# Attention kernel: q's and k's weights loaded by SP, idle products from ones, ACT's parts of the forms after the step's exponentials, another tail for the last group

## The chip, the cores and the metric

The kernel runs on one core of one Trainium2 chip. The metric is the device time of one launch in microseconds (us), median of several runs. Its engines: PE (TensorE, matrix products, with its weight loads PEld), DVE (VectorE), ACT (ScalarE), POOL (GpSimd) and SP (SyncE, which only issues transfers here). Each engine works through its own list of instructions in order; semaphores hold an instruction back until another engine or a transfer has got far enough.

## The reference

Four images of 64 x 64 positions and 256 channels. Without the parts that are not called:

```python
q = jnp.einsum('bwhc,cd->bwhd', x, Wq) + bq      # 128 channels
k = jnp.einsum('bwhc,cd->bwhd', x, Wk) + bk      # 128 channels
v = jnp.einsum('bwhc,cd->bwhd', x, Wv) + bv      # 256 channels
pq, pk, pv = (t.reshape(B, -1, N) for t in (q, k, v))   # N = 4096
energy = jnp.einsum('bcn,bcm->bnm', pq, pk)      # 4096 x 4096 for each image
attention = jax.nn.softmax(energy, axis=-1)
out = jnp.einsum('bcm,bnm->bcn', pv, attention)
return gamma * out.reshape(B, W, H, C) + x
```

All of it is float32.

## The kernel before

The large products run on PE in a faster type (fp32r) that keeps fewer bits, so each float32 operand is split into parts, here called its forms: an upper part h, made by ACT with a multiplication by a number just under 1, and two more, made by DVE out of h and the operand (`scalar_tensor_tensor`). `halved` (L260) makes the forms of q and k, `halve_v` (L288) those of v (vh, vl, vd), `upper` and `halves` those of the exponentials.

For each image there is first a projection phase of 16 tiles i. `transposed(i)` loads a tile of x by SP, transposes it on PE (L124), and ACT copies it out (L130). `project_qk(b, i)` (L271) makes q and k on PE (L137), DVE adds the bias (qks, L146), POOL stores q to DRAM (L275), `halved` makes k's forms (ACT L263, DVE L266), and POOL stores these (L279). `project_v` does the same for v (PE L158, ACT L167 and L292, DVE L296); the v forms of the last two tiles are left for the steps.

Then follow 128 steps u: 16 groups g of 256 columns n, and in each group 8 steps t, each over 512 rows m. A step u works on several stages at once:

- `energy(b, u + 3, k)` for k = 0 and 1: six products on PE into the PSUM banks sa and sb (L330; two banks each, taken in turn), then two exponentials on ACT, x from sa and y from sb (L334).
- `join(b, u + 2)`: x = x * y on DVE (L344); `upper(b, u + 2)`: h on ACT (L349). Both stand between the energies of k = 0 and those of k = 1.
- `halves(b, u + 1)`: l and d on DVE (L355, L358).
- `attend(b, u)`: 24 products on PE into the accumulators acc (two banks a0, a1, of h and l) and the shared bank bb (of d) (L380). vh and vl carry two columns of ones, so that column C of an accumulator is the sum of the exponentials, Z.

At each step with `ahead % 8 == 5` q's forms for the next group are made (`halve_q`); in steps 1 and 3 of an image the v forms that were left. Both are generators in two pieces: the ACT part (L263, L292) stands right after the energies of k = 0, ahead of h; the DVE parts (L266, L296) stand at the end of the step, after `halves`.

After a group's last step ACT takes the accumulators out into o (L391), and `finish` does the rest in pieces, one for each `proceed()`: DVE takes Z, its reciprocal times gamma and adds bb (L404 to L406); ACT scales o (L409); PE transposes o into ot (L417); DVE adds it to x (L421); POOL stores the result (L422). `begin` and the list of `proceed()` calls fix where each piece stands between the other work. At the end of an image the pieces of its last group fall into the next image's first projections:

```python
            if b + 1 < B:
                proceed()
                images[b + 1].transposed(1)
                proceed()
                project_qk(b + 1, 0)
```

In the order of PE's list the next image's transposes of tile 2, the transposes ot of the last group, and q and k of tile 1 then follow one another.

The very last group has its own tail, `finish_last` (L440): Z from both accumulators, factors r and ra on DVE, ACT scales bb, DVE adds the scaled accumulators (L455), PE transposes, DVE adds to x (L465), SP stores. `guard` (L424) checks that all Z lie between two limits and writes the flag `again`; every engine reads it at L561 and would run a general path, which these inputs do not take.

At the start, ACT issues the loads of Wq and Wk (L90, L91), POOL those of the biases, Wv and gamma, SP those of x. PE makes 12 idle transposes of the identity (L199), which POOL has to build first.

Of the kernel before, what the change touches and what calls it, by code (L numbers as in the profile page):

```python
# [9 lines left out]
F32 = mybir.dt.float32  # L10
# [3 lines left out]
ALU = mybir.AluOpType  # L14
# [6 lines left out]
def kernel(  # L21
# [65 lines left out]
    ones = const.tile([P, P], F32, name="ones")  # L87
    nc.vector.memset(ones, 1.0)
    wqk_sb = const.tile([P, KC, 2 * C2], F32, name="wqk_sb")
    nc.scalar.dma_start(wqk_sb[:, :, :C2], wq.rearrange("(k p) d -> p k d", p=P))  # L90
    nc.scalar.dma_start(wqk_sb[:, :, C2:], wk.rearrange("(k p) d -> p k d", p=P))  # L91
    bqk_sb = const.tile([P, 2 * C2], F32, name="bqk_sb")
    nc.gpsimd.dma_start(bqk_sb[:, :C2], bq.partition_broadcast(P))
    nc.gpsimd.dma_start(bqk_sb[:, C2:], bk.partition_broadcast(P))
# [100 lines left out]

    with tc.tile_pool(name="ps_w", bufs=1, space=PSUM) as ps_w:
        wp = ps_w.tile([P, P], F32, name="wp")
        for _ in range(12):
            nc.tensor.transpose(wp, ident, ident)  # L199

    with ExitStack() as fast:
        fast.enter_context(tc.manual_schedule())
# [57 lines left out]
        def halved(f, x):  # L260

            h = f[:, :, 0, :]
            nc.scalar.activation(h, x, AF.Identity, scale=UPPER / 64)  # L263
            yield
            for j, s, op in ((1, -64.0, ALU.add), (2, 64.0 * (1.0 + E), ALU.subtract)):
                nc.vector.scalar_tensor_tensor(  # L266
                    f[:, :, j, :], h.bitcast(F32), s, x, ALU.mult, op
                )
            yield

        def project_qk(b, i):  # L271
            images[b].qk(i)
            x = now["qk"]
            for s in range(2):
                nc.gpsimd.dma_start(qd[b, i // 2 + NG // 2 * s][:, i % 2, :], x[:, s, :C2])  # L275
            f = kpool.tile([P, 2, 3, P], F32R, tag="f", name=f"f_{b}_{i}", bufs=2)
            for _ in halved(f, x[:, :, C2:]):
                pass
            nc.gpsimd.dma_start(kf[b, i // 2][:, i % 2], f.rearrange("p s j d -> p s (j d)"))  # L279

        def project_v(b, i):
            images[b].v(i)
            units[b, "v4", i] = now["v4"]
            if i < NI - 2:
                for _ in halve_v(b, i):
                    pass

        def halve_v(b, i):  # L288
            v4 = units.pop((b, "v4", i))
            m = slice(2 * i, 2 * i + 2)  # L290
            h = vh[:, m, :C]
            nc.scalar.activation(h, v4, AF.Identity, scale=UPPER * E)  # L292
            yield

            for t, f in ((vl, 1.0 / E), (vd, 1.0 / E + 1.0)):
                nc.vector.scalar_tensor_tensor(  # L296
                    t[:, m, :C], h.bitcast(F32), -f, v4, ALU.mult, ALU.add
                )
            yield

        def load_q(b, g):
            t = work.tile([P, NJ, P], F32, tag="qr", name=f"qr_{b}_{g}", bufs=1)
# [2 lines left out]

        def halve_q(b, g):
            t = work.tile([P, 3, NJ, P], F32R, tag="q", name=f"q_{b}_{g}")
            loads[b, "q", g] = t
            yield from halved(t.rearrange("p f j d -> p j f d"), loads.pop((b, "qr", g)))

        def load_k(b, u):
            if u < STEPS:
# [80 lines left out]
        def factors(b, g, gamma):  # L393

            r = work.tile([P, 2, NJ], F32, tag="r", name=f"r_{b}_{g}")
            nc.vector.reciprocal(r[:, 0, :], zall[:, b * NG + g, :])
            nc.vector.tensor_tensor(r[:, 0, :], r[:, 0, :], gamma.to_broadcast([P, NJ]), ALU.mult)
            return r[:, 0, :], r[:, 1, :]

        def finish(b, g, o, bb, xr):  # L400
            yield
            yield

            nc.vector.tensor_copy(zall[:, b * NG + g, :], o[:, :, C])  # L404
            r, _ = factors(b, g, gam1)
            nc.vector.tensor_tensor(o[:, :, :C], o[:, :, :C], bb, ALU.add)  # L406
            yield
            for j in range(NJ):
                nc.scalar.activation(  # L409
                    o[:, j, :C], o[:, j, :C], AF.Identity, scale=r[:, j : j + 1]  # L410
                )
            yield
            yield
            tp = ps_t.tile([P, 2, NB], F32, tag="t", name=f"ot_{b}_{g}")
            for s in range(2):
                for j in range(NJ):
                    nc.tensor.transpose(  # L417
                        tp[:, s, j * P : (j + 1) * P], o[:, j, s * P : (s + 1) * P], ident
                    )
            yield  # L420
            nc.vector.tensor_tensor(xr, xr, tp, ALU.add)  # L421
            nc.gpsimd.dma_start(ov[b, g], xr)  # L422

        def guard():  # L424

            z = zall.rearrange("p n j -> p (n j)")
            ok = ppool.tile([P, 4, NB], F32, tag="y", name="ok")[:, 0, : B * NG * NJ]
            nc.vector.tensor_scalar(ok, z, Z_LOW, None, ALU.is_ge)
            nc.vector.scalar_tensor_tensor(ok, z, Z_HIGH, ok, ALU.is_le, ALU.mult)
            yield  # L430
            nc.vector.tensor_reduce(zs, ok, AX.X, ALU.min)
            nc.vector.tensor_scalar(zs, zs, 0.5, None, ALU.is_lt)
            zp = ps_s.tile([P, 1], F32, tag="b", name="zp")
            nc.tensor.matmul(zp, ones, zs, start=True, stop=True)
            yield
            nc.vector.tensor_copy(again, zp)
            yield
            yield

        def finish_last(b, g, xr):  # L440

            for j in range(NJ):
                a = now["acc"][j]
                nc.vector.tensor_copy(zall[:, b * NG + g, j : j + 1], a[:, C : C + 1])
            r, ra = factors(b, g, gam)
            check = guard()
            nc.vector.tensor_scalar(ra, r, 1.0 + E, None, ALU.mult)
            o = work.tile([P, NJ, C + 2], F32, tag="o", name=f"o_{b}_{g}")
            tps = []
            for j in range(NJ):  # L450
                next(check)
                nc.scalar.activation(
                    o[:, j, :C], now["bb"][:, j, :], AF.Identity, scale=r[:, j : j + 1]
                )
                nc.vector.scalar_tensor_tensor(  # L455
                    o[:, j, :C], now["acc"][j][:, :C], ra[:, j : j + 1], o[:, j, :C], ALU.mult, ALU.add
                )
                tp = (ps_t, ps_s)[j].tile([P, 2, P], F32, tag="ta"[j], name=f"ot_{b}_{g}_{j}")
                for s in range(2):
                    nc.tensor.transpose(tp[:, s, :], o[:, j, s * P : (s + 1) * P], ident)  # L460
                tps.append(tp)
            for j in range(NJ):
                next(check)
                n = slice(j * P, (j + 1) * P)
                nc.vector.tensor_tensor(xr[:, :, n], xr[:, :, n], tps[j], ALU.add)  # L465
            nc.sync.dma_start(ov[b, g], xr)

        def begin(b, i):

            if i == 5:  # L470
                load_q(b, 0)
            if i == 9:
                for _ in halve_q(b, 0):
                    pass
            if i in (4, 6, 8):
                load_k(b, i // 2 - 2)
            if i >= 10:
                energy(b, (i - 10) // 2, i % 2)
            if i in (12, 14):
                join(b, i // 2 - 6)  # L480
            if i in (13, 15):
                upper(b, i // 2 - 6)
                load_k(b, i // 2 - 3)

        image(0)
        for b in range(B):
            pr = images[b]
            if b == 0:
                now["banks"] = energies
                pr.transposed(0)  # L490
                pr.transposed(1)
                project_qk(b, 0)
            for i in range(1, NI):
# [13 lines left out]
            for u in range(STEPS):  # L507
# [182 lines left out]
```

## Time and profile before

| | us |
|---|---|
| median of 3 runs | 2453.45 (2453.05 to 2455.39) |
| the profiled execution | 2453.05 |
| its span, first to last instruction | 2451.3 |
| PE, PEld busy | 2438.7, 2408.0 |
| DVE, ACT, POOL busy | 2099.0, 1795.2, 424.5 |

The mean TensorE clock that was granted is 0.999 of full speed. A row of the timeline has the start in us from the span's start, the duration, the engine, the line, the operation, out<-in with shapes, how many instructions are merged, and in brackets how long the engine stood idle before and what released it. An ACT or DVE instruction can start a little before the last one has ended.

### The profile page before, as it was taken

To read this page: it belongs to the slowest core of one execution; us is meant where nothing else is said; L and a number is where in the kernel's file an instruction comes from. 1 tells how busy PE (TensorE), PEld (TensorE's weight loads), DVE (VectorE), ACT (ScalarE), POOL (GpSimd) and SP (SyncE) were. 2 spreads that over 40 slices of the span, in tenths; PEclk is the share of its full clock that TensorE was granted. 3 is DMA by queue.
4 is the path that set the end of the run, shared out by engine and by line. 5 is a ranking of instruction groups with operands and counts; after the bars stand their busy time and mean duration, and the time that the engine had idled before them with its cause. 6 is when DMAs were issued, how large, how long until landed. Compare 5 with 4: busy or idle time off the path is not lost.

```text
span 2451.3 us, 50024 instructions
## 1 busy us (share of the span) xinstructions
PE 2438.7 (99%) x19982; PEld 2408.0 (98%) x19982; DVE 2099.0 (86%) x2314; ACT 1795.2 (73%) x3201; POOL 424.5 (17%) x781
## 2 busy tenths in 40 slices
PE   9999999999999999999999999999999999999998
PEld 8999999999899999999989999999998999999998
DVE  5988888888698888888869888888886988888887
ACT  5777777776677777777667777777766777777775
POOL 4211111111411111111141111111114111111110
PEclk9999999999999999999999999999999999999999
DMA  7766666665776666666477666666647766666663
GB/s 234 224 202 209 204 207 202 202 215 153 235 221 197 210 203 208 208 197 213 141 243 226 203 203 202 208 210 201 206 140 248 223 204 201 204 207 210 203 202 111
DMA packets 137407, 498.92 MB, mean 204 GB/s; under 512 B 15536, under 2 KB 57264, under 8 KB 137168
## 3 DMA queue, kind: packets, MB, share of 16 engines
q0 software_dynamic: 92320, 453.17, 60.0%
q1 hardware_dynamic: 44304, 42.22, 5.5%
q8 instruction: 160, 2.62, 0.4%
q14 instruction: 79, 0.65, 0.1%
q10 hardware_dynamic: 544, 0.26, 0.0%
HBM read 445.25 MB, written 50.33 MB: 202 GB/s over the span
## 4 chain that ended last, share of the span: by engine, by line


## 5 line engine op out<-in xcount | busy, mean ns | idle before, releaser
L334 ACT ACTIVATE x<-sa 128x512 f32<-128x512 f32 x1024 | 612.2, 598 | 516.1 <-PE sa L330 514.0
L344 DVE TENSOR_TENSOR x<-x,y 128x1024 f32<-128x1024 f32 x512 | 626.2, 1223 | 234.4 <-ACT y L334 234.4
L330 PE MATMUL sa<-q,k 128*128 128x256 f32 x4096 | 735.4, 279 | 0.0
L358 DVE SCALAR_TENSOR_TENSOR d<-h,x 128x1024 fp32r<-128x1024 f32 x512 | 623.3, 1217 | 0.0
L355 DVE TENSOR_TENSOR l<-x,h 128x1024 fp32r<-128x1024 f32 x512 | 623.2, 1217 | 0.0
L330 PEld LDWEIGHTS sa<-q,k 128*128 128x128 f32 x4096 | 619.4, 188 | 0.4
L334 ACT ACTIVATE y<-sb 128x512 f32<-128x512 f32 x1024 | 615.7, 601 | 0.0
L380 PE MATMUL a<-vh,h 128*128 128x258 f32 x4096 | 574.4, 283 | 0.0
L380 PE MATMUL a<-vl,l 128*128 128x258 f32 x4096 | 572.8, 282 | 0.0
L330 PE MATMUL sb<-q,k 128*128 128x256 f32 x2048 | 567.1, 277 | 0.0
L380 PE MATMUL bb<-vd,d 128*128 128x256 f32 x4096 | 558.6, 279 | 0.0
L314 POOL DMA_DIRECT2D k<-kf x512 | 279.1, 545 | 1573.3 <-PE sb L330 1548.3
L349 ACT ACTIVATE h<-x 128x1024 fp32r<-128x1024 f32 x512 | 543.8, 1062 | 8.3 <-DVE x L344 7.8
L380 PEld LDWEIGHTS a<-vl,l 128*128 128x128 f32 x4096 | 525.3, 189 | 0.0
L380 PEld LDWEIGHTS a<-vh,h 128*128 128x128 f32 x4096 | 522.9, 189 | 0.0
L380 PEld LDWEIGHTS bb<-vd,d 128*128 128x128 f32 x4096 | 515.1, 188 | 0.0
L330 PEld LDWEIGHTS sb<-q,k 128*128 128x128 f32 x2048 | 384.5, 188 | 0.1
L137 PE MATMUL qk<-wqk_sb,xts 128*128 128x256 f32 x512 | 121.0, 379 | 0.0
L158 PE MATMUL v<-xts,wv_sb 128*128 128x256 f32 x512 | 120.3, 379 | 0.0
L158 PEld LDWEIGHTS v<-xts,wv_sb 128*128 128x128 f32 x512 | 97.3, 190 | 13.2
L137 PEld LDWEIGHTS qk<-wqk_sb,xts 128*128 128x128 f32 x512 | 92.3, 190 | 10.0
L275 POOL DMA_DIRECT2D qd<-qks x128 | 69.2, 549 | 179.8 <-DVE qks L146 170.6
(56 smaller groups left out, 864.4 us busy)
## 6 DMA issues: line engine op xcount, KB each, us to landing
k<-kf POOLq DMA_DIRECT2D x512, 768.0 KB, 4.7
x<-in_x_dram SPq DMA_DIRECT2D x128, 256.0 KB, 3.9
kf<-f POOLq DMA_DIRECT2D x64, 384.0 KB, 4.0
out_dram<-x POOLq DMA_DIRECT2D x63, 256.0 KB, 2.5
qd<-qks POOLq DMA_DIRECT2D x128, 64.0 KB, 3.0
qr<-qd SPq DMA_DIRECT2D x64, 128.0 KB, 3.6
wv_sb<-in_L_conv_Wv_dram POOLq DMA_DIRECT2D x1, 256.0 KB, 5.7
out_dram<-x SPq DMA_DIRECT2D x1, 256.0 KB, 3.8
```

The source lines that it names most:

```text
L137: nc.tensor.matmul(qk[:, s, :], self.xt[i][:, k, s, :], wqk_sb[:, k, :], start=(k == 0), stop=(k == KC - 1),)
L158: nc.tensor.matmul(vp[:, eh, :], wv_sb[:, k, eh * P : (eh + 1) * P], self.xt[i][:, k].rearrange("p s a -> p (s a)"), start=(k == 0), stop= ...
L275: nc.gpsimd.dma_start(qd[b, i // 2 + NG // 2 * s][:, i % 2, :], x[:, s, :C2])
L314: nc.gpsimd.dma_start(t.rearrange("p (i s) f d -> p i s (f d)", s=2), kf[b, u % NU])
L330: nc.tensor.matmul(to[:, i], kt[:, 2 * k + i, f, :], q[:, f], start=first, stop=last)
L334: nc.scalar.activation(to[:, 2 * k : 2 * k + 2, :], sp.rearrange("p i j d -> p i (j d)"), AF.Exp, scale=scale,)
L344: nc.vector.tensor_tensor(x, x, y, ALU.mult)
L349: nc.scalar.activation(h, units[b, u], AF.Identity, scale=UPPER)
L355: nc.vector.tensor_tensor(l, x, h.bitcast(F32), ALU.subtract)
L358: nc.vector.scalar_tensor_tensor(d, h.bitcast(F32), 1.0 + E, x, ALU.mult, ALU.subtract)
L380: nc.tensor.matmul(out_, left[:, i, j * P : (j + 1) * P], right[:, m, : out_.shape[1]], start=(t == i == 0 and (left is h or left is d and ...
```

## The change

- SP issues the loads of Wq and Wk, after its first tile of x and before its second.
- PE's idle work is 7 matrix products of the tile of ones with itself instead of the 12 transposes, and two more of them between the transposes of the first and the second tile.
- `halved` and `halve_v` are plain functions: ACT's part and DVE's parts of q's and v's forms are made together at the end of the step, so that ACT's part comes after both pairs of exponentials.
- At the end of an image `project_qk(b + 1, 0)` comes ahead of the second `proceed()`, the one in which ACT scales o.
- In the last group ACT scales the two accumulators, DVE scales and adds bb; the comparison of the guard is one operation on POOL (`max` and `min`) and one on DVE (`is_equal`), and its product zp comes after the transposes.

```diff
-    nc.scalar.dma_start(wqk_sb[:, :, :C2], wq.rearrange("(k p) d -> p k d", p=P))
-    nc.scalar.dma_start(wqk_sb[:, :, C2:], wk.rearrange("(k p) d -> p k d", p=P))
...
         wp = ps_w.tile([P, P], F32, name="wp")
-        for _ in range(12):
-            nc.tensor.transpose(wp, ident, ident)
+        for _ in range(7):
+            nc.tensor.matmul(wp, ones, ones, start=True, stop=True)
...
             h = f[:, :, 0, :]
             nc.scalar.activation(h, x, AF.Identity, scale=UPPER / 64)
-            yield
             for j, s, op in ((1, -64.0, ALU.add), (2, 64.0 * (1.0 + E), ALU.subtract)):
...
-            yield
...
             nc.scalar.activation(h, v4, AF.Identity, scale=UPPER * E)
-            yield
...
+            halved(t.rearrange("p f j d -> p j f d"), loads.pop((b, "qr", g)))
             loads[b, "q", g] = t
-            yield from halved(t.rearrange("p f j d -> p j f d"), loads.pop((b, "qr", g)))
...
             ok = ppool.tile([P, 4, NB], F32, tag="y", name="ok")[:, 0, : B * NG * NJ]
-            nc.vector.tensor_scalar(ok, z, Z_LOW, None, ALU.is_ge)
-            nc.vector.scalar_tensor_tensor(ok, z, Z_HIGH, ok, ALU.is_le, ALU.mult)
-            yield
+            nc.gpsimd.tensor_scalar(ok, z, Z_LOW, Z_HIGH, ALU.max, ALU.min)
+            nc.vector.tensor_tensor(ok, ok, z, ALU.is_equal)
             nc.vector.tensor_reduce(zs, ok, AX.X, ALU.min)
-            nc.vector.tensor_scalar(zs, zs, 0.5, None, ALU.is_lt)
             zp = ps_s.tile([P, 1], F32, tag="b", name="zp")
             nc.tensor.matmul(zp, ones, zs, start=True, stop=True)
-            yield
-            nc.vector.tensor_copy(again, zp)
...
+            return zp
...
         def finish_last(b, g, xr):
 
+            r = work.tile([P, 2, NJ], F32, tag="r", name=f"r_{b}_{g}")
+            o = work.tile([P, NJ, C + 2], F32, tag="o", name=f"o_{b}_{g}")
+            acc, bb = now["acc"], now["bb"]
             for j in range(NJ):
-                a = now["acc"][j]
-                nc.vector.tensor_copy(zall[:, b * NG + g, j : j + 1], a[:, C : C + 1])
-            r, ra = factors(b, g, gam)
-            check = guard()
-            nc.vector.tensor_scalar(ra, r, 1.0 + E, None, ALU.mult)
-            o = work.tile([P, NJ, C + 2], F32, tag="o", name=f"o_{b}_{g}")
+                rj, raj, z = r[:, 0, j : j + 1], r[:, 1, j : j + 1], acc[j][:, C : C + 1]
+                nc.vector.reciprocal(rj, z)
+                nc.vector.tensor_tensor(raj, rj, gam1, ALU.mult)
+                nc.scalar.activation(o[:, j, :C], acc[j][:, :C], AF.Identity, scale=raj)
+                nc.vector.tensor_tensor(rj, rj, gam, ALU.mult)
+            for j in range(NJ):
+                nc.vector.tensor_copy(zall[:, b * NG + g, j : j + 1], acc[j][:, C : C + 1])
             tps = []
             for j in range(NJ):
-                next(check)
-                nc.scalar.activation(
-                    o[:, j, :C], now["bb"][:, j, :], AF.Identity, scale=r[:, j : j + 1]
-                )
                 nc.vector.scalar_tensor_tensor(
-                    o[:, j, :C], now["acc"][j][:, :C], ra[:, j : j + 1], o[:, j, :C], ALU.mult, ALU.add
+                    o[:, j, :C], bb[:, j, :], r[:, 0, j : j + 1], o[:, j, :C], ALU.mult, ALU.add
                 )
...
+            zp = guard()
             for j in range(NJ):
-                next(check)
                 n = slice(j * P, (j + 1) * P)
                 nc.vector.tensor_tensor(xr[:, :, n], xr[:, :, n], tps[j], ALU.add)
+                if j == 0:
+                    nc.vector.tensor_scalar(again, zp, P - 0.5, None, ALU.is_lt)
             nc.sync.dma_start(ov[b, g], xr)
...
                 now["banks"] = energies
+                pr.load(0)
+                nc.sync.dma_start(wqk_sb[:, :, :C2], wq.rearrange("(k p) d -> p k d", p=P))
+                nc.sync.dma_start(wqk_sb[:, :, C2:], wk.rearrange("(k p) d -> p k d", p=P))
                 pr.transposed(0)
+
+                wp = ps_t.tile([P, P], F32, tag="t", name="wp1")
+                for _ in range(2):
+                    nc.tensor.matmul(wp, ones, ones, start=True, stop=True)
                 pr.transposed(1)
...
-                beside = []
-                if ahead // NU + 1 < NG and ahead % NU == 5:
-                    beside.append(halve_q(b, ahead // NU + 1))
-                if u in (1, 3):
-                    beside.append(halve_v(b, NI - 2 + u // 2))
                 for k in range(2):
                     if ahead < STEPS:
                         energy(b, ahead, k)
-                    if k == 0:
-                        for forms in beside:
-                            next(forms)
                     if k == 0 and u + 2 < STEPS:
                         join(b, u + 2)
                         upper(b, u + 2)
...
                 if u + 1 < STEPS:
                     halves(b, u + 1)
-                for forms in beside:
-                    next(forms)
+                if ahead // NU + 1 < NG and ahead % NU == 5:
+                    halve_q(b, ahead // NU + 1)
+
+                if u in (1, 3):
+                    halve_v(b, NI - 2 + u // 2)
                 attend(b, u)
...
                 proceed()
                 images[b + 1].transposed(1)
+                project_qk(b + 1, 0)
                 proceed()
-                project_qk(b + 1, 0)
```

More of the change, by code (lines that the diff above doesn't have):

```diff
@@ L276, in project_qk @@
             f = kpool.tile([P, 2, 3, P], F32R, tag="f", name=f"f_{b}_{i}", bufs=2)
-            for _ in halved(f, x[:, :, C2:]):
-                pass
+            halved(f, x[:, :, C2:])
             nc.gpsimd.dma_start(kf[b, i // 2][:, i % 2], f.rearrange("p s j d -> p s (j d)"))
@@ L284, in project_v @@
             if i < NI - 2:
-                for _ in halve_v(b, i):
-                    pass
+                halve_v(b, i)
         def halve_v(b, i):
@@ L391, in attend @@
                     nc.scalar.activation(o[:, j, :], acc[j], AF.Identity, scale=1.0 + E)
[L393 to L398, printed above, removed]
         def finish(b, g, o, bb, xr):
@@ L404, in finish @@
             nc.vector.tensor_copy(zall[:, b * NG + g, :], o[:, :, C])
-            r, _ = factors(b, g, gam1)
+            r = work.tile([P, 2, NJ], F32, tag="r", name=f"r_{b}_{g}")[:, 0, :]
+            nc.vector.reciprocal(r, zall[:, b * NG + g, :])
+            nc.vector.tensor_tensor(r, r, gam1.to_broadcast([P, NJ]), ALU.mult)
             nc.vector.tensor_tensor(o[:, :, :C], o[:, :, :C], bb, ALU.add)
@@ L427, in guard @@
             ok = ppool.tile([P, 4, NB], F32, tag="y", name="ok")[:, 0, : B * NG * NJ]
-            nc.vector.tensor_scalar(ok, z, Z_LOW, None, ALU.is_ge)
-            nc.vector.scalar_tensor_tensor(ok, z, Z_HIGH, ok, ALU.is_le, ALU.mult)
-            yield
+            nc.gpsimd.tensor_scalar(ok, z, Z_LOW, Z_HIGH, ALU.max, ALU.min)
+            nc.vector.tensor_tensor(ok, ok, z, ALU.is_equal)
             nc.vector.tensor_reduce(zs, ok, AX.X, ALU.min)
-            nc.vector.tensor_scalar(zs, zs, 0.5, None, ALU.is_lt)
             zp = ps_s.tile([P, 1], F32, tag="b", name="zp")
             nc.tensor.matmul(zp, ones, zs, start=True, stop=True)
-            yield
-            nc.vector.tensor_copy(again, zp)
-            yield
-            yield
+            return zp
         def finish_last(b, g, xr):
+            r = work.tile([P, 2, NJ], F32, tag="r", name=f"r_{b}_{g}")
+            o = work.tile([P, NJ, C + 2], F32, tag="o", name=f"o_{b}_{g}")
+            acc, bb = now["acc"], now["bb"]
             for j in range(NJ):
-                a = now["acc"][j]
-                nc.vector.tensor_copy(zall[:, b * NG + g, j : j + 1], a[:, C : C + 1])
-            r, ra = factors(b, g, gam)
-            check = guard()
-            nc.vector.tensor_scalar(ra, r, 1.0 + E, None, ALU.mult)
-            o = work.tile([P, NJ, C + 2], F32, tag="o", name=f"o_{b}_{g}")
+                rj, raj, z = r[:, 0, j : j + 1], r[:, 1, j : j + 1], acc[j][:, C : C + 1]
[5 more added lines that the diff above has]
+                nc.vector.tensor_copy(zall[:, b * NG + g, j : j + 1], acc[j][:, C : C + 1])
             tps = []
             for j in range(NJ):
-                next(check)
-                nc.scalar.activation(
-                    o[:, j, :C], now["bb"][:, j, :], AF.Identity, scale=r[:, j : j + 1]
-                )
                 nc.vector.scalar_tensor_tensor(
-                    o[:, j, :C], now["acc"][j][:, :C], ra[:, j : j + 1], o[:, j, :C], ALU.mult, ALU.add
+                    o[:, j, :C], bb[:, j, :], r[:, 0, j : j + 1], o[:, j, :C], ALU.mult, ALU.add
                 )
@@ L472, in begin @@
             if i == 9:
-                for _ in halve_q(b, 0):
-                    pass
+                halve_q(b, 0)
             if i in (4, 6, 8):
```

## The prediction

> **What bounds the kernel now.** I read the page's busy times first, then the waits by total, then the timeline in four places: the start, an image's first steps, the seam between two images, the end.
>
> ```profile
> PE 2438.7 (99%) x19982; PEld 2408.0 (98%) x19982; DVE 2099.0 (86%) x2314; ACT 1795.2 (73%) x3201; POOL 424.5 (17%) x781
> ```
>
> TensorE (PE) is busy for 2438.7 of 2451.3 us. The 12.6 us without it lie at the two ends: its first transposes of x start at 5.31, its last product of step 127 ends at 2440.88. In between the waits by total name no wait of PE but one for x (0.8 us, in the start). So two things set the time: what PE does at the ends, and any new wait that the change puts into PE's in-order stream. Nothing on ACT, DVE or POOL counts until it reaches PE. The waits that show how much room there is:
>
> ```profile
> ACT x L334 <- PE sa L330: 514.0, 496, 1.7
> DVE x L344 <- ACT y L334: 234.4, 416, 0.7
> ACT h L349 <- DVE x L344: 7.8, 8, 1.4
> ```
>
> ACT has about 1.0 us of room in a step, DVE 0.56. ACT's h waits for DVE's join only 8 times: twice an image, at its start and its end.
>
> **The seams between images (three).** Timeline before, first to second image:
>
> ```profile
> 616.24 0.91 ACT L409 ACTIVATE o<-o,r 128x256 f32<-128x256 f32 x2
> 617.29 0.60 PE L124 MATMUL xt<-ident,x 128*128 128x128 f32 x4
> 617.49 0.69 DVE L146 TENSOR_TENSOR qks<-qk,bqk_sb 128x512 f32<-128x512 f32 x1 [1.48 <-PE qk L137]
> 617.73 0.60 PE L417 MATMUL ot<-ident,o 128*128 128x128 f32 x4
> 618.16 1.89 PE L137 MATMUL qk<-wqk_sb,xts 128*128 128x256 f32 x8
> 618.22 0.42 ACT L263 ACTIVATE f<-qks 128x256 fp32r<-128x256 f32 x1 [1.06 <-DVE qks L146]
> 618.54 0.57 ACT L130 COPY xts<-xt 128x512 f32<-128x512 f32 x1
> ```
>
> Before, ACT scales o (L409) at 616.24, while it has nothing else to do, and PE finds o ready at 617.73. The change puts project_qk ahead of the piece that scales, so on ACT the scales stand behind f of L263, and f waits for DVE's qks until 618.22. PE's order stays as it was: xt, ot, qk of the next tile. So PE now stands in front of ot. Replay: f at 618.22, the first scale 0.32 later (as L130 follows f now) at 618.54, ending 0.53 later at 619.07; the second starts 0.38 after the first (0.91 for both less 0.53) and ends at 619.45. The first transpose waits for the first scale, the second for the second; from ACT or DVE to PE takes 0.06 (an o of DVE ends at 2441.90, its transpose starts at 2441.96). Transposes at 619.13, 619.51, 619.62, 619.73, then qk at 619.84 instead of 618.16: 1.68 us. Queued behind the wait on PE are qk and all the rest of the image; no later idle time of PE gives it back. The other two seams show the same spacings (scales 1.48 before ot, f 1.97 behind the scales). 3 x 1.68 = 5.04. Bounds: nothing if ot found o ready all the same; 1.9 each (5.7) if the second scale takes a full 0.53 after the first.
>
> **ACT's parts of the q and v forms.** 60 q parts (L263) and 8 v parts (L292) move behind the second pair of exponentials. DVE's order is unchanged, but its forms (L266, L296) now wait for an ACT part that ends later. Two places differ.
>
> In 56 of the 60 q steps the step stands alone. From the step at 150 us: without q in front, h starts at 151.58 instead of 151.89, the exponentials end at 153.60, q at 153.90; DVE's q forms start at 153.93 instead of 152.99 and the next join at 154.60 instead of 153.95. The join after that waited 0.38 for y; it starts 0.2 late, and the lag is gone a step later. PE's banks are free earlier than before in that step. Cost 0. The cover is DVE's room of 0.2 to 0.7 a step and the step of lead of l and d; without it 0.65 x 56 = 36 us.
>
> At an image's start a v, a q and a v part come in three steps running, while DVE has no room left from the projections. Before, second image:
>
> ```profile
> 698.62 0.68 DVE L296 SCALAR_TENSOR_TENSOR vl<-vh,v 128x512 fp32r<-128x512 f32 x1
> 699.83 1.21 DVE L344 TENSOR_TENSOR x<-x,y 128x1024 f32<-128x1024 f32 x1
> 701.07 1.06 ACT L349 ACTIVATE h<-x 128x1024 fp32r<-128x1024 f32 x1 [0.61 <-DVE x L344]
> 702.04 0.58 ACT L334 ACTIVATE x<-sa 128x512 f32<-128x512 f32 x1
> 702.51 0.59 ACT L334 ACTIVATE y<-sb 128x512 f32<-128x512 f32 x1
> 703.52 0.39 PE L330 MATMUL sa<-q,k 128*128 128x256 f32 x2
> 703.75 0.28 PE L330 MATMUL sb<-q,k 128*128 128x256 f32 x1
> ```
>
> Replay of the three steps. First: h waits for its join (ends 687.74), exponentials 688.72 and 689.19, v part 689.67 to 690.30; DVE was free for the v forms at 689.93 and starts at 690.33, 0.40 late. Second: join 691.53, h 692.77, exponentials 693.74 and 694.21, q 694.69 to 695.11; the q forms start at 695.14 instead of 694.54, 0.60 late. Third: join 695.81, h 697.06, exponentials 698.00 and 698.48, v part 698.96 to 699.59; the v forms start at 699.62 instead of 698.62, 1.00 late. The join of 699.83 so starts at 700.83, h at 702.07, the exponentials end at 703.62 and 704.10. PE's sa (703.52) and sb (703.75) overwrite the banks that these read: sa goes at 703.68, sb at 704.16, 0.41 late. The lag then shrinks by 0.6 a step. The other images have the same rows (h waited 0.60, 0.61, 0.60, 0.61). 4 x 0.41 = 1.64. Bounds: 0 if the lag is 0.4 smaller than replayed; 0.65 each (2.6) if each of the three hand-overs costs 0.08 more. l and d are no danger: they are ready 2.9 us ahead of PE and come 1.0 late.
>
> **The start.**
>
> ```profile
> 5.31 0.79 PE L124 MATMUL xt<-ident,x 128*128 128x128 f32 x4
> 6.92 0.66 PE L124 MATMUL xt<-ident,x 128*128 128x128 f32 x4 [0.83 <-DMA x<-in_x_dram]
> ```
>
> From 6.92 on PE never waits, so only the landing of the second x counts. ACT's two loads (issues of 0.42 and 0.49) go to SP between the first x (issued at 0.73, landed 3.5 later) and the second (issued at 1.48, landed 5.4 later, 6.88). SP issues the second x about 1.0 later, and the third too. But the DMA engines are 0.8 to 1.15 busy from 2 us on, and the same 768 KB (two x, two weights) have to pass before the second x is whole; POOL's loads beside them stay. I take 0; bounds +1.0 (the issue shift in full) and -0.9 (issued at 2.5 and landing in 3.5, as the first x did: 6.0).
>
> The row says that the second x waits for shared engines, not for its issue. [...]
>
> The idle products: a product of fp32 is two records here (zp of L434 is one matmul, x2), so 7 are 14 records. The 12 transposes before took 0.22 each, where four xt later need 0.11: PE runs at half rate until about 5.6. From the ones (ready at 1.00) 14 x 0.22 end at about 4.1, the first x's transposes and two more products end by 5.9; PE is as busy ahead of 5.6 as before, and the second x still comes last. Cost 0, bounds -0.2 and +2 (4 us of work at half rate).
>
> **The end.**
>
> ```profile
> 2440.92 0.84 ACT L452 ACTIVATE o<-bb,r 128x256 f32<-128x256 f32 x2 [6.77 <-PE bb L380]
> 2442.91 0.75 DVE L465 TENSOR_TENSOR x<-x,ot 128x256 f32<-128x256 f32 x2
> 2443.68 0.60 SPq L466 DMA_DIRECT2D out_dram<-x  x1
> ```
>
> Now ACT scales both accumulators before bb is done: they close at 2439.50 and 2439.97, reciprocal and product take 0.2 each, so o is ready at 2440.36 and 2440.81. DVE adds bb at 2440.92 and 2441.32, transposes follow at 2441.46 and 2441.85. The comparison on POOL (bounds 0.22 and 0.32, its other elementwise rows, for 128 columns) ends near 2441.0 and waits for nobody. DVE's two guard operations 2441.72 to 2442.2, first add to 2442.56, again after zp at about 2442.66, second add to 2443.16: the store goes out 0.5 earlier. The rest (SP's load of again, its branch, the barrier) follows SP. -0.5; bounds -0.8 and 0 (the second add behind a later zp).
>
> **Sum.** 5.04 + 1.64 + 0 - 0.5 = +6.2. The profiled execution took 2453.05 (span 2451.3), so 2459.2; the median of the runs is 0.4 higher: 2459.6. About 0.2%, 4.9 us, is what a measurement of this kernel can tell from no change.
>
> **Rivals.** (A) Not slower: the seam does not reach PE, because o's scales are done before 617.84 after all, or because PE takes up qk first. The place is L417, the price 5.04; it decides if more than a quarter of the wait goes. For it: only the record of ACT's order speaks of the wait. Against: f cannot start before 618.22. Time 2454.6. (B) The lag at the image starts stays under the 0.6 to 0.7 that PE's banks had to spare: 2458.0, just inside 0.2%. For it: the margin is 0.41 of a replay over three steps; against: all four images have the same rows. (C) The second x lands with its issue, 1.0 later: 2460.6. For it: it starts behind three loads of the same queue; against: the busy engines. (D) PE stays at half rate past the second x: 2461.6.
>
> **Chances.** The sum as it stands 0.57, A 0.07, B 0.14, C 0.15, D 0.05, something faster that no row shows 0.02. Range 2457.4 to 2461.4: it takes in B, C and the bounds of the end, and leaves out A, most of D and the faster rest. Slower by over 0.2%: the sum, C, D and a little of B, 0.80; within 0.2%: A and most of B, 0.18; faster 0.02.
>
> **What would show it.** Right: PE idle before ot by about 1.3 us at three seams, L409 behind L263; a short idle of PE before sb in the fifth step of each image; the second xt near 6.9; the store 0.5 earlier from PE's last product. Wrong: no wait of PE on ACT's o, or a first xt row at half rate after 7 us.

## The result: 11.5 us slower, and the profile after

The changed kernel took 2464.91 us (median of 6 runs, 2464.33 to 2465.69) against 2453.45 for the kernel before on the same chip: ratio 1.0045, 95% interval 1.0032 to 1.0058. Its profiled execution took 2465.06, with a span of 2462.9. On a second chip the pair gave 2466.4 against 2455.84, again 1.0045 (1.0028 to 1.0061).

The page's busy times and the waits by total (us in total, times, longest us):

```profile
PE 2445.1 (99%) x19988; PEld 2411.2 (98%) x19988; DVE 2095.2 (85%) x2315; ACT 1803.6 (73%) x3201; POOL 425.5 (17%) x782
```

```profile
ACT x L326 <- PE sa L322: 493.5, 484, 1.7
DVE x L336 <- ACT y L326: 188.4, 304, 0.7
...
ACT h L341 <- DVE x L336: 19.2, 16, 1.6
...
PE ot L404 <- ACT o L396: 3.6, 3, 1.2
...
PE xt L122 <- DMA x<-in_x_dram: 2.4, 1, 2.4
...
PE sa L322 <- ACT x L326: 1.0, 4, 0.3
```

ACT and DVE wait less than before (493.5 instead of 514.0, 188.4 instead of 234.4), which buys nothing. PE has two waits that it did not have, three times on o at the seams (line `ot`) and four times on ACT's exponentials (line `sa`), and its wait for x grew from 0.8 to 2.4. ACT's h now waits 16 times for the join, not 8.

I matched PE's instructions of the two traces one by one. The lag is how much later an instruction starts in the changed kernel. It grows at the start, at the seams and image starts, and at the end. From an image's first steps to the next seam it stays the same within 0.03; in each projection phase it drifts by 0.1 at most, 0.2 to 0.3 in all:

| place | lag added | predicted |
|---|---|---|
| start, up to the third x | 2.79 | 0 |
| four image starts, 0.77 to 0.82 each | 3.2 | 1.64 |
| three seams, 1.70 each | 5.1 | 5.04 |
| end | 0.23 | -0.5 |
| sum | 11.3 | 6.2 |

With the drift this is the 11.6 by which the span grew.

**A seam**, in the timeline (start us, length us, engine, line, operation, idle time before and what ended it):

```profile
621.82 0.42 ACT L261 ACTIVATE f<-qks 128x256 fp32r<-128x256 f32 x1 [1.87 <-DVE qks L144]
622.15 0.89 ACT L396 ACTIVATE o<-o,r 128x256 f32<-128x256 f32 x2
622.69 0.95 PE L404 MATMUL ot<-ident,o 128*128 128x128 f32 x4 [1.19 <-ACT o L396]
...
623.48 1.89 PE L135 MATMUL qk<-wqk_sb,xts 128*128 128x256 f32 x8
```

The scales of o stand behind f, PE stands 1.19 in front of ot, and the four transposes take 0.95 instead of 0.60, as the second pair waits for the second scale. Less the lag of 3.61 that stood there before, ot starts 1.35 late and the projection behind it 1.71 late.

**The second image's fifth step:**

```profile
705.13 0.69 DVE L289 SCALAR_TENSOR_TENSOR vl<-vh,v 128x512 fp32r<-128x512 f32 x1 [0.41 <-ACT vh L286]
...
706.35 1.22 DVE L336 TENSOR_TENSOR x<-x,y 128x1024 f32<-128x1024 f32 x1
707.66 1.06 ACT L341 ACTIVATE h<-x 128x1024 fp32r<-128x1024 f32 x1 [1.58 <-DVE x L336]
...
709.25 0.50 PE L322 MATMUL sa<-q,k 128*128 128x256 f32 x2 [0.23 <-ACT x L326]
...
709.74 0.19 PEld L322 LDWEIGHTS sb<-q,k 128*128 128x128 f32 x1 [0.19 <-ACT y L326]
709.74 0.38 PE L322 MATMUL sb<-q,k 128*128 128x256 f32 x1
```

DVE waits for the v part, its join is late, so is h, so are the exponentials, and PE waits for both banks, for sb with the weight load of its product.

**The start**, and a table of two stretches of it (stretch, its length, busy time of PE, PEld, DVE, ACT and POOL with the instructions in brackets, granted clock, DMA share, GB/s):

```profile
8.04 1.09 PE L122 MATMUL xt<-ident,x 128*128 128x128 f32 x4 [2.38 <-DMA x<-in_x_dram]
8.93 3.17 PE L135 MATMUL qk<-wqk_sb,xts 128*128 128x256 f32 x8
11.93 0.60 PE L122 MATMUL xt<-ident,x 128*128 128x128 f32 x4
```

```profile
4.70:8.10 3.40, 1.02 (x9) 0.83 (x9) 0.00 (x0) 0.59 (x1) 0.57 (x2) 1.00 0.97 284
8.10:11.50 3.40, 3.40 (x11) 2.84 (x12) 0.00 (x0) 0.59 (x1) 0.46 (x2) 0.50 0.49 141
```

The second x's transposes start at 8.04 instead of 6.92. They and the first projection then run at a granted clock of 0.50: 1.09 instead of 0.66 and 3.17 instead of 1.89. Before, the second xt was followed by the projection at full clock, and the third xt started 2.22 after the second; now it starts 3.89 after it.

**The end:**

```profile
2452.34 0.16 DVE L434 COPY zall<-a 128x1 f32<-128x1 f32 x1 [0.32 <-ACT o L431]
...
2452.59 0.65 POOL L415 TENSOR_SCALAR ok<-zall 128x128 f32<-128x128 f32 x1 [19.73 <-DVE zall L434]
...
2454.42 0.16 DVE L449 TENSOR_SCALAR again<-zp 128x1 int32<-128x1 f32 x1 [0.21 <-PE zp L419]
...
2454.50 0.41 DVE L447 TENSOR_TENSOR x<-x,ot 128x256 f32<-128x256 f32 x1
...
2454.94 0.60 SPq L450 DMA_DIRECT2D out_dram<-x  x1
```

Counted from the start of bb's last product (2440.60 before, 2451.98 now), the store goes out at 2.96 instead of 3.08, but `again` is made at 2.44 instead of 2.22, its first readers follow at 2.63 instead of 2.41, and the span ends at 10.90 instead of 10.67.

### The profile page after: what moved, and what is told of

Read it like the earlier page. It is cut to its first block, busy times and chain, and to the rows that moved or that the text cites. A ratio compares the mean times of both kernels' runs of the same rounds, so it can differ in the third digit from the quotient of the medians.

```text
span 2462.9 us, 50040 instructions
## 1 busy us (share of the span) xinstructions
PE 2445.1 (99%) x19988; PEld 2411.2 (98%) x19988; DVE 2095.2 (85%) x2315; ACT 1803.6 (73%) x3201; POOL 425.5 (17%) x782
## 3 DMA queue, kind: packets, MB, share of 16 engines
q8 instruction: 160, 2.62, 0.4%
## 4 chain that ended last, share of the span: by engine, by line
PE 96%; ACT 2%; DVE 1%; issue 0%; DMA 0%; SPq 0%; ACTq 0%; DVEq 0%
PE a L372 39%; PE bb L372 19%; PE sa L322 18%; PE sb L322 9%; PE qk L135 5%; PE v L156 4%; PE ot L404 1%; PE xt L122 1%; ACT h L341 1%; DVE x L336 1%; ACT x L326 0%; ACT y L326 0%; DVE vd L289 0%; DMA x<-in_x_dram 0%; ACT vh L286 0%
## 5 line engine op out<-in xcount | busy, mean ns | idle before, releaser
L326 ACT ACTIVATE x<-sa 128x512 f32<-128x512 f32 x1024 | 612.5, 598 | 496.6 <-PE sa L322 493.5
L336 DVE TENSOR_TENSOR x<-x,y 128x1024 f32<-128x1024 f32 x512 | 625.8, 1222 | 188.4 <-ACT y L326 188.4
```

The lines of the kernel that those rows point to most:

```text
L326: nc.scalar.activation(to[:, 2 * k : 2 * k + 2, :], sp.rearrange("p i j d -> p i (j d)"), AF.Exp, scale=scale,)
L336: nc.vector.tensor_tensor(x, x, y, ALU.mult)
```

## The experiments

The theory after the result: four separate costs add up, at the start (landing and clock), at the image starts (the forms' order), at the seams (project_qk ahead of the scales) and, small, at the end. The rivals: the start is a matter of the landing alone; the clock's drop is an accident of one run; the image starts come from the q parts, or from the v parts alone. Each run undoes one thing or does one thing alone. The runs come in three groups, each on a chip of its own, so each is read against the kernel before on that chip (2455.02 for seam_back to idle_long, 2455.84 for before_again to best, 2455.79 for v_early to idle_only). The changed kernel itself ran on the second of these chips only; on the others its place is an estimate by its ratio of 1.0045.

**seam_back**: the projection follows the piece that scales, as before.

```diff
-                project_qk(b + 1, 0)
                 proceed()
+                project_qk(b + 1, 0)
```

> The changed kernel with one edit undone: at an image's end the piece in which ACT scales o stands again ahead of project_qk. Theory (PE waits at ot for scales that stand behind f on ACT): the jump at the three seams goes, 1.65 to 1.75 us each, so the time falls by 5.0 to 5.3 us, to about 2459.7, and the trace has no idle PE before ot. Rival (the wait only moves: f and what hangs on it come later and hold PE elsewhere, or the image's first steps take back what the seam gives): under 2 us of gain.

Measured: 2461.3 (2460.31 to 2462.32), ratio 1.0023 (1.0013 to 1.0032). By the changed kernel's ratio, that kernel would stand at 2455.02 x 1.0045 = 2466.1 on this chip, so the seams give 4.8. In the trace all three seam jumps are gone and the image starts stay at 0.75 to 0.82. Timeline, first seam:

```profile
621.64 0.91 ACT L396 ACTIVATE o<-o,r 128x256 f32<-128x256 f32 x2
...
623.12 0.60 PE L404 MATMUL ot<-ident,o 128*128 128x128 f32 x4
...
623.61 0.42 ACT L261 ACTIVATE f<-qks 128x256 fp32r<-128x256 f32 x1 [1.07 <-DVE qks L144]
```

The scales end ahead of ot, whose four take 0.60 again with no wait, and f comes last.

**forms_back**: ACT's q and v parts between the two energies again.

```diff
+                beside = []
+                if ahead // NU + 1 < NG and ahead % NU == 5:
+                    beside.append(halve_q(b, ahead // NU + 1))
+                if u in (1, 3):
+                    beside.append(halve_v(b, NI - 2 + u // 2))
                 for k in range(2):
                     ...
+                    if k == 0:
+                        for forms in beside:
+                            next(forms)
...
-                if ahead // NU + 1 < NG and ahead % NU == 5:
-                    halve_q(b, ahead // NU + 1)
-                if u in (1, 3):
-                    halve_v(b, NI - 2 + u // 2)
+                for forms in beside:
+                    next(forms)
```

> The changed kernel with one edit undone: ACT's parts of q's and v's forms stand again between the two pairs of exponentials. Theory (the lag of DVE over an image's first steps reaches ACT's exponentials, and PE waits for the banks sa and sb in the fifth step): the four jumps of 0.82 us go, the time falls by 3.3 us to about 2461.6, nothing changes in the other 56 q steps. Rival (the late q parts cost in every group a little that no single gap shows): a gain well over 3.3 us, up to 60 x 0.1 = 6 us more.

Measured: 2463.03 (2462.3 to 2463.59), ratio 1.0030 (1.0019 to 1.0041), some 3.1 below where the changed kernel would stand. All four jumps at image starts are gone, the three seams stay at 1.70, and h's wait for the join is back at 8 times, 7.9 us.

**weights_act**: ACT issues the loads of Wq and Wk at the start; the rest as changed.

```diff
-                nc.sync.dma_start(wqk_sb[:, :, :C2], ...)
-                nc.sync.dma_start(wqk_sb[:, :, C2:], ...)
...
+    nc.scalar.dma_start(wqk_sb[:, :, :C2], ...)
+    nc.scalar.dma_start(wqk_sb[:, :, C2:], ...)
```

> The changed kernel with one edit undone: ACT issues the loads of Wq and Wk at the start; idle products stay 7 and 2. Theory (the second x landed 1.1 us later because three loads of SP stand ahead of it, and PE's idle time until then lost it the full clock for 3.4 us): the second xt starts at about 6.9 instead of 8.04; if the clock stays full, the first step starts 2.8 us earlier and the time is about 2462.1; if the clock is lost all the same, only 1.1 us are won, about 2463.8. Rival (the landing is set by the bytes in flight, not by who issues them): the second xt stays near 8.0 and the time near 2464.9.

Measured: 2464.9 (2462.74 to 2466.39), ratio 1.0036 (1.0025 to 1.0047). The eight runs fall into two groups, three at 2462.74 to 2462.87 and five at 2464.81 to 2466.39. The traced run, of the second group, has its second xt at 8.23, while the other kernels of this group of runs, with SP's loads, have it at 9.3 to 9.85. That is 1.1 to 1.6 earlier than in those, but not near the 6.9 that was expected: on its own it would fit the rival's 8.0 as well. It still ran at half rate from 8.82 to 12.23. That the first group is the one that kept its clock is likely from the 2 us between the groups, but no trace of it was taken.

**idle_long**: 13 idle products instead of 2 between the first two x.

```diff
-                for _ in range(2):
+                for _ in range(13):
                     nc.tensor.matmul(wp, ones, ones, start=True, stop=True)
```

> The changed kernel with 13 instead of 2 idle products between the transposes of the first and the second tile, so that PE is busy until the second x lands near 8.04. Theory (PE's 2.4 us without work cost it the full clock from 8.1 to 11.5): the clock stays full, the second xt still starts at 8.0 to 8.1, the rest of the start is 1.7 us shorter, time about 2463.2. Rival (half rate there has another cause, such as the phase of the clock or products of ones that do not count as work): no change, 2464.9, with matmul rows at half rate after 8 us.

Measured: 2464.75 (2464.42 to 2465.3), ratio 1.0037 (1.0023 to 1.0051), some 1.3 below where the changed kernel would stand. Timeline:

```profile
9.52 0.66 PE L122 MATMUL xt<-ident,x 128*128 128x128 f32 x4 [0.78 <-DMA x<-in_x_dram]
...
11.74 0.60 PE L122 MATMUL xt<-ident,x 128*128 128x128 f32 x4
```

From the second xt to the third 2.22 pass; in seam_back and forms_back, on the same chip, 3.91 and 3.80. So the clock is a cost of its own, 1.6 to 1.7 in the traces, and PE's idle time ahead of the second xt is what brings it. All seven traces of kernels with two products there (PE idle for 2.2 to 4.0 ahead of the second xt) ran the first projection at half rate, with a mean granted clock of 0.998 over the span, and all five with 6 to 13 (idle for 1.83 at most) ran it at full clock, with a mean of 0.999, so it is not an accident of one run. The landing is as late as ever.

**before_again** and **after_again**: both kernels unchanged on a second chip.

> The kernel before, unchanged, for its trace beside the three others on the same chip. Theory (the second x lands by its place among SP's loads, and the clock follows how busy PE was): second xt about 1.1 us earlier than in the unchanged changed kernel on this chip, and half rate over by about 6 us. Rival (the landing differs from chip to chip more than between the kernels): both second xt within 0.3 us of one another.

> The changed kernel, unchanged, for its start on the same chip as the others. Theory: second xt 1.1 us later than in the kernel before, half rate for one stretch of 3.4 us after it, first step 2.8 us later, seams 3 x 1.70 and image starts 4 x 0.82 as on the first chip; about 11 us above the kernel before.

The kernel before took 2456.15 in this run. Its timeline:

```profile
7.91 1.12 PE L124 MATMUL xt<-ident,x 128*128 128x128 f32 x4 [1.48 <-DMA x<-in_x_dram]
8.82 3.31 PE L137 MATMUL qk<-wqk_sb,xts 128*128 128x256 f32 x8
```

It too can run its first projection at half rate: 3.31 instead of 1.89, and the third xt at 11.97 is 2.82 later than in the trace that the prediction was made from. Neither the half rate that was expected to be over by 6 us nor the 2.8 between the two kernels came about here. (The profile has no record of a clock ahead of 11.68 in this run and prints 1.00 there; the lengths of the rows show the half rate.) In the same place the changed kernel had its second xt at 9.41, 1.50 after that of before, and its third at 13.24, 1.27 after. So the later landing is a cost with both kernels at half rate; the clock's part of the start is one that the kernel before pays in some runs and not in others.

**x1_first**: SP loads both x first, then the weights; 6 idle products instead of 2 on PE, which start at 4.97, behind the issue of the second x at 1.48.

```diff
+                pr.load(1)
                 nc.sync.dma_start(wqk_sb[:, :, :C2], ...)
                 nc.sync.dma_start(wqk_sb[:, :, C2:], ...)
...
-                for _ in range(2):
+                for _ in range(6):
```

> The changed kernel with SP's loads in the order first x, second x, Wq, Wk, third x, and 6 instead of 2 idle products between the first two tiles. Theory (the place on SP's queue sets the landing): second xt 1.0 to 2.0 us earlier than in the unchanged changed kernel; the first qk then waits for Wk, whose landing moves behind, so the first step gains at most 1 us from the order, and 1.7 us more if the clock stays full. Rival (the bytes of POOL's loads beside them set it): second xt as late as in the changed kernel.

Measured: 2463.84 (2463.47 to 2464.2), ratio 1.0035 (1.0022 to 1.0047). Timeline:

```profile
7.36 0.66 PE L122 MATMUL xt<-ident,x 128*128 128x128 f32 x4 [0.88 <-DMA x<-in_x_dram]
...
8.95 1.97 PE L135 MATMUL qk<-wqk_sb,xts 128*128 128x256 f32 x8 [0.94 <-DMA wqk_sb<-in_L_conv_Wk_dram]
```

The second x comes 2.05 before that of after_again, and ahead of all seven traces in which SP loads the weights first (8.04 to 9.85), so its place in SP's queue moves its landing. It was issued 1.14 earlier (1.48 instead of 2.62); no run separates the time of the issue from the order in the queue. The clock stayed full with the 6 products. What is late next is Wk: the projection waits 0.94 for it.

**best**: weights on ACT, seam and forms as before; of the change only the idle products (7, then 8) and the new end.

```diff
+    nc.scalar.dma_start(wqk_sb[:, :, :C2], ...)   # and Wk; seam and forms as in the two runs above
...
-                for _ in range(2):
+                for _ in range(8):
```

> Only the idle products and the tail of the changed kernel: the seam's order, ACT's parts of the forms and ACT's loads of the weights as in the kernel before; 7 idle products of ones, then 8 more between the first two tiles. Theory (the three undone edits are the whole loss, the tail is worth 0.1, a busy PE ahead of the second x holds the clock): no jump at seams and image starts, start within 0.5 us of the kernel before's on this chip, time equal to the kernel before's or up to 0.5 us under it. Rival (the tail or the products cost something of their own): 1 us or more above it.

Measured: 2454.74 (2454.06 to 2456.63), ratio 0.9997 (0.9988 to 1.0007), no different from the kernel before. There is no jump at any seam or image start. The third xt starts at 10.82, 1.15 ahead of that of before_again, where at most 0.5 was expected: this run kept the full clock and before_again did not.

**v_early** and **q_early**: only the v parts, or only the q parts, back between the energies. Against forms_back:

```diff
-                    beside.append(halve_q(b, ahead // NU + 1))   # v_early; q_early: halve_v
+                    behind.append(halve_q(b, ahead // NU + 1))
```

> The changed kernel with ACT's v parts (steps 1 and 3 of an image) back between the two pairs of exponentials; the 60 q parts stay late. Theory (it takes the late v, q and v parts together to push the lag past what the banks sa and sb have to spare): no jump, or less than 0.3 us, in PE's fifth step of an image; seams as before at 1.70. Rival (the late q part alone makes PE wait): the four jumps stay at 0.5 us or more.

> The changed kernel with ACT's q parts back between the two pairs of exponentials; the v parts of steps 1 and 3 stay late. Theory (lags add up over three steps): two late v parts leave a lag of 0.6 to 0.9 us at the fifth step, so the jumps shrink to between 0 and 0.4 us. Rival (only the last late part, v in step 3, counts): the jumps stay at 0.8 us.

Measured (one run each, so without an interval): 2464.06 and 2465.54. The late q parts alone cost nothing at the image starts (0.0 four times, h waits for the join 12 times); the late v parts alone cost 0.47 to 0.49 (h waits 16 times), more than I expected; both together 0.82. So the v parts carry the loss, and the q part between them costs something only together with these.

**pool_late**: best, and POOL's loads of bq, bk and Wv go behind those of bv and gamma.

```diff
-    nc.gpsimd.dma_start(bqk_sb[:, :C2], bq.partition_broadcast(P))   # and bk, Wv
...
+    nc.gpsimd.dma_start(bqk_sb[:, :C2], bq.partition_broadcast(P))   # and bk, Wv, behind gamma
```

> The kernel of only idle products (7 and 8) and the new tail, with POOL's three large loads (both biases of q and k, Wv) issued after its three small ones, about 1.7 us later. Theory (POOL's broadcast of the biases shares the DMA engines with the first two tiles and the weights, and holds back the second x): the second xt starts 0.5 to 1.5 us earlier than in the run of only idle products, near 7.0 us, and the first step with it. Rival (only the order on each queue counts): the second xt stays between 8 and 8.6.

**idle_only**: the kernel before, with its own end, and the idle products alone changed.

```diff
-        for _ in range(12):
-            nc.tensor.transpose(wp, ident, ident)
+        for _ in range(7):
+            nc.tensor.matmul(wp, ones, ones, start=True, stop=True)
...
                 pr.transposed(0)
+                wp = ps_t.tile([P, P], F32, tag="t", name="wp1")
+                for _ in range(8):
+                    nc.tensor.matmul(wp, ones, ones, start=True, stop=True)
                 pr.transposed(1)
```

> The kernel before with one thing added: idle products of ones, 7 at the start and 8 between the first two tiles; its own tail. Theory (the new tail costs 0.23 us because the flag again comes 0.22 later, and the flag's readers, not the store, set the end): from bb's last product to the span's end 10.67 to 10.69 us, against 10.90 with the new tail; full clock from the second xt on; time equal to the kernel before's or up to 1.5 us under it. Rival (the store sets the end): 10.9 or more.

Measured: pool_late 2454.33 (2453.45 to 2454.48), ratio 0.9996 (0.9986 to 1.0005); idle_only 2454.32 (2453.56 to 2454.62), ratio 0.9994 (0.9984 to 1.0004). The second xt started at 6.90 in pool_late, 8.22 in idle_only, yet the medians agree. The traced run of pool_late is the fastest of its ten and that of idle_only the second slowest, so these two starts need not be typical, and that POOL's loads hold back the second x rests on one trace. Both are clearly faster than the changed kernel and lie 1.5 under the median of before, which the intervals do not tell from nothing. All ten runs of each end below 2454.7, where the kernel before reached from 2453.61 to 2457.11 on that chip; but best, with the same idle products, reached 2456.63 on the second chip, so a narrower spread is not shown in general. From the start of bb's last product to the end of the span, idle_only, with the old end, takes 10.68; all kernels with the new end take 10.90 or 10.91.

## Why the prediction was wrong, point by point

**Seams: right.** 1.68 each predicted, 1.70 measured, and seam_back takes them away. f did stand ahead of the scales, PE did stand in front of ot, nothing gave it back. Rival A fell.

**The 56 lone q steps: right.** Cost 0; from an image's first steps to the next seam, where these steps lie, the lag stays the same within 0.03, and with the q parts alone late (v_early) it does too.

**Image starts: the mechanism right, the size half.** The failing step is the replay of three steps. Less the 5.31 that the whole kernel already lagged there (2.79 + 0.82 + 1.70), DVE's three forms start 0.43, 0.71 and 1.20 late where the replay had 0.40, 0.60 and 1.00, and h of the fifth step is 1.28 late instead of 1.00. Most of it is the hand-over from join to h: a join that ends at 706.35 + 1.22 = 707.57 releases an h at 707.66, so 0.09 passes where I used 0.03, three times over (0.18 of the 0.28). The 0.03 was measured, at the same place in the kernel before (join 699.83, h 701.07). But that kernel has the longer gap too, at its image ends:

```profile
605.72 1.22 DVE L344 TENSOR_TENSOR x<-x,y 128x1024 f32<-128x1024 f32 x1 [0.74 <-ACT y L334]
...
607.04 1.06 ACT L349 ACTIVATE h<-x 128x1024 fp32r<-128x1024 f32 x1 [1.35 <-DVE x L344]
```

In the changed kernel every h for which ACT stood and waited has 0.09. Why the place changed from one gap to the other stays open. All this makes sb 0.68 late instead of 0.41, just past the 0.65 that I had named as the bound. The second piece was in no bound: before, the weight load of sb started 0.11 ahead of its product, beside the product in front of it (703.64 and 703.75). After the wait both start at 709.74, and the product stands 0.38 instead of 0.28.

```profile
703.64 0.19 PEld L330 LDWEIGHTS sb<-q,k 128*128 128x128 f32 x1
```

0.41 + 0.27 + 0.11 = 0.79, and behind this step the lag is 6.10, 0.79 above the 5.31. Rival B fell.

**Start, the landing: wrong.** The failing step is "I take 0": the second x, I argued, waits for shared engines and not for its issue. SP issued it at 2.62 instead of 1.48, and it was at PE at 8.04 instead of 6.92: 5.4 from issue to PE in both. 1.1 here, 1.5 on the second chip: rival C, which I gave 0.15. x1_first shows the same from the other side. That the 5.4 is the same twice is luck in part: on the second chip it is 6.4 for the kernel before and 6.8 for the changed one. Over all traces the second xt starts at 9.3 on average where SP loads the weights first (seven traces) and at 8.0 where ACT loads them and POOL's loads stand as before (five). The DMA engines were as busy as I said (0.97 of the stretch from 4.70 to 8.10), but equal bytes in all did not make the second x land at the same time.

**Start, the idle products: wrong.** The failing step looked only at the time ahead of 5.6 ("PE is as busy ahead of 5.6 as before") and not at the gap behind it. With two products after the first x, PE was busy 1.02 of the 3.40 us from 4.70, then ran at 0.50 for the next 3.4: 1.67 more up to the third x. Its bound of +2 and rival D (0.05) had about the size but another path, a half rate that lasts from the beginning; here the clock was full from 4.68 and was lost again. idle_long shows the cause. The two terms are also tied: the later x made up 1.1 of the 2.38 for which PE stood idle ahead of the second xt, and the clock was lost there, so C and D should not have been priced as if only one could come.

In the trace of the changed kernel the granted clock changes at 4.68, 8.10 and 11.51, 3.41 apart: full from 4.68, 0.50 from 8.10, full again from 11.51.

**End: wrong sign, small.** Two steps failed. "The rest (...) follows SP": from the flag's readers to the end of the span 8.26 pass in both kernels, from the store 7.59 and 7.94, so the end went with the flag. And "The comparison on POOL (...) ends near 2441.0 and waits for nobody": the second copy of zall waited for ACT's o, the comparison started 0.61 after the start of bb's last product, and took 0.65, where I bounded it at 0.22 to 0.32 by rows of POOL that do something else or have 2 columns. On DVE the second add stands behind `again`, which waited for zp and so for this comparison; that is why the store gained 0.12 and not 0.5. The flag came 0.22 later, the end 0.23 later. Each kernel with the new end repeats it, and from the flag's readers to the end 8.26 to 8.28 pass in all fourteen traces.

**The sum.** Misses: 2.8 at the start, 1.6 at the image starts, 0.7 at the end, 5.1 together; the time lay 5.3 above the forecast, and 3.5 above the upper end of the range. The range let C and D stand as alternatives and put no weight on several bounds at their upper ends at once.

## What to carry to other kernels

An engine that runs in order pays for what stands ahead of the piece that PE needs next (1.70 us at each seam here), so before a small piece is moved behind another one, find its reader on the bottleneck and count. Around a wait, price the released instruction's own weight load (0.11 here), and each hand-over with the longest gap that the trace shows for this pair of engines (0.09 from join to h instead of 0.03 here), since chains without room add these up. At a start that hangs on a load, count the load's place in its queue (1.1 to 2.05 us here), and look at how busy TensorE is in the gap behind its first work, not only ahead of it: 1.02 of 3.40 us busy went with a clock of 0.50 here, 2.78 of 3.41 with the full clock.

## What the runs showed of the hardware that was not expected

- An idle time of 2.22 us can go with the loss of the full clock. PE busy for 1.02 of a 3.40 us stretch (4.70 to 8.10 in the changed kernel, longest idle 2.38) lost it, as did 1.19 of 3.41 in weights_act (5.41 to 8.82, longest idle 2.22); 2.18 of 3.42 in best (7.36 to 10.78, behind an idle time of 1.83) and 2.78 of 3.41 in idle_only (5.91 to 9.32) kept it. Between 1.19 and 2.18 there is only before_again, which had half rate already and still had it after 1.86 of 3.40 (4.85 to 8.25).
- The moments at which the clock changes differ from run to run of one kernel (half rate ends at 11.51 in one run of the changed kernel, at 12.7 in another; the kernel before reached full clock at 5.62 in one run and at 11.68 in another). One trace of a start is therefore one draw, worth 2.8 us here.
- The landing of the second x differs between runs by more than an issue: from 6.92 to 8.60 where ACT loads the weights, from 8.04 to 9.85 where SP loads them ahead of it. With POOL's two broadcasts and Wv issued later it was 6.90, in one trace. Why it varies stays open.
